# One block's adjacency by four indirect transfers of GpSimd, its features by four transfers addressed from registers

## The chip, the core and the metric

The kernel runs on one core of a Trainium2 chip. The core has five engines, each with an instruction queue of its own: TensorE (PE in the profile; the loads of its weights are listed as PEld), VectorE (DVE), ScalarE (ACT), GpSimd (POOL) and SyncE (SP), which here only issues transfers. Sixteen DMA engines move data between the chip's memory (HBM) and the core's on-chip memory (SBUF); TensorE writes to PSUM. The engines run independently and wait for each other and for transfers at semaphores. The metric is the device time of one execution in microseconds.

## The reference

One layer of a message-passing network over 128 graphs of 64 nodes with 128 features each. For each ordered pair of nodes (i, j) a three-layer MLP makes a message from the two nodes' features; messages are summed over j where the adjacency has an edge; a second MLP updates each node.

```python
def _mlp(x, w0, b0, g0, be0, w1, b1, g1, be1, w2, b2):
    h = jax.nn.relu(x @ w0 + b0)
    h = _layernorm(h, g0, be0)
    h = jax.nn.relu(h @ w1 + b1)
    h = _layernorm(h, g1, be1)
    return h @ w2 + b2
...
pair_feats = jnp.concatenate([f_i, f_j], axis=-1)          # (128, 64, 64, 256)
messages = _mlp(pair_feats, msg_w0, ..., msg_b2)
messages = messages * coupling_matrix[..., None]           # adj: (128, 64, 64), 0 or 1
agg = jnp.sum(messages, axis=2)
upd_in = jnp.concatenate([part_feats, agg], axis=-1)
updated = part_feats + _mlp(upd_in, upd_w0, ..., upd_b2)   # x: (128, 64, 128)
```

About an eighth of the adjacency's entries are edges, so a kernel may work on edges alone.

## The kernel before

**Tiling.** The kernel lists the edges of each graph in slots, 640 per graph (`CAP`), and works on edges alone. Two graphs make a pair (64 pairs, `NP`), four pairs a block (16 blocks, `NB`, `PB` = 4). A chunk is 512 edges; a pair has 2.5 chunks, a block ten, the whole run 160 (`NCHK`). If a graph has too many edges, a dense path behind a flag computes everything again; with these inputs it isn't taken.

**A block's way.** Its adjacency `an` (128 partitions: two graphs of 64 rows; by 4 pairs by 64 columns) is loaded in `load_adj`, its features `xn` (128 partitions by 4 pairs by 128) in `load_x`. From `an`, VectorE counts edges along each row (`rank`, tile `rk`), and GpSimd works out each edge's place (`place`, `place_out`, tile `posall`). From `xn`, TensorE makes transposes (`turn_x`, tile `xnT`) and then two products per node, split into a low and a high part (`rows`, tiles `abl` and `abh`). For each pair the two selection matrices that say which nodes an edge joins are made: `node_rows` casts one on GpSimd (tile `i`), `marks` and `compare` make the other on TensorE and VectorE (tile `j`). Four transfers of `stack`, two `s<-i` and two `s<-j` (one of each per graph of the pair), put them together in a tile `s` with 128 partitions. `gather` multiplies `abl` and `abh` by `s` (tile `hps`), chunk by chunk, which gives the first layer's output for 512 edges. The rest of the MLP, the sums over edges (tiles `oh` and `w`, `ys`) and the node update (`uo`) follow; the features `xn` are used once more in `residual`, which adds them to the output. GpSimd also makes a seed `u` for the second layer of some chunks, which VectorE adds in `y`.

**What sets the order.** Each step is put in a list by `at(n, tag, fn, ...)` at a time of 144 units per chunk plus a correction from the table `WHEN`, and the list is sorted and written out in that order. Each engine runs its own instructions in that order; so does SyncE with the transfers. `load_adj` of block b is at 19 chunks ahead of the block, `load_x` at 12 ahead, with corrections. Blocks 0 and 1 are loaded ahead of the list; `load_adj` and `load_x` handle blocks 2 to 15, 14 calls each. A steady block takes about 29.35 us. In the rows of the profile that carry a line number, L719 is the adjacency load, L724 the feature load, L898 `stack`, L1018 the transposing transfer of `node_marks`, L1162 the store of the output, L933 `gather`, L908 `marks`, L819 `turn_x`, and L1621 the load of the flag into a register on each engine at the end.

Of the kernel before, what the change touches and what calls it, by code (L numbers as in the profile page):

```python
# [12 lines left out]
I32 = mybir.dt.int32  # L13
# [362 lines left out]
def tile_gnn(  # L376
# [40 lines left out]
    nc = tc.nc  # L417
    B, N, C = x.shape
    P = 128
# [5 lines left out]
    NP = B // 2  # L425
# [5 lines left out]
    PB = 4  # L431
# [12 lines left out]
    xf = x.rearrange("b n c -> (b n) c")  # L444
    of = out.rearrange("b n c -> (b n) c")
    adjp = adj.rearrange("(p g) i j -> (g i) p j", g=2)

    const = ctx.enter_context(tc.tile_pool(name="const", bufs=1))
# [25 lines left out]
    def load_first(b, q0, q1):  # L474
# [55 lines left out]
    nc.gpsimd.iota(slot, pattern=[[2, CAP]], base=1, channel_multiplier=0,  # L530
                   allow_small_or_imprecise_dtypes=True)

    posall = const.tile([P, 2, PB, 2, N], F16, name="posall")
    nc.vector.memset(posall, 0.0)
    ones_row = const.tile([1, P], F32, name="ones_row")
# [134 lines left out]
    def edge_path(es):  # L670
# [45 lines left out]

        def load_adj(b):
            an = blkp.tile([P, PB, N], F32, name="an", bufs=3)
            nc.sync.dma_start(an, adjp[:, b * PB:(b + 1) * PB, :])  # L719
            blocks[b]["an"] = an  # L720

        def load_x(b):
            xn = blkp.tile([P, PB, C], F32, name="xn", bufs=5)
            nc.sync.dma_start(xn, xf[b * PB * P:(b + 1) * PB * P, :]  # L724
                              .rearrange("(q p) c -> p q c", p=P))
            blocks[b]["xn"] = xn

        def rank(b):
# [454 lines left out]
        for b in range(NB):  # L1183
            o = b * CPB
            if b > 1:
                at(max(o - 19, 0), "", load_adj, b)
                at(max(o - 12, 0), "", load_x, b)
            if b > 0:
                r = max(o - 12, 1)
                at(max(o - 14, 0), "", rank, b)  # L1190
                at(r, "", count, b)
                at(r + 1, "", count_out, b)
                at(r + 1, "", degrees, b)
                at(max(o - 9, r + 1), "", place, b)
                at(r + 2 if b == 1 else o - 7, "", place_out, b)
                at(max(o - 7, 13), "", odd_weights, b)
                at(o - 4, "", turn_x, b)
                at(o - 3, "", turn_x_out, b)
            for half, n in ((0, o - 3 if b else -1), (1, o + 2 if b else 3)):
                if n >= 0:  # L1200
                    if b < 2:
                        at(n, f".{half}", rows, b, half)
                    elif half == 0:
                        at(o - 2, "", rows_both, b)
                    r = o - 1 if b > 1 else n + 1
                    at(r, f".{half}", rows_hi, b, half)
                    at(r, f".{half}", rows_lo, b, half)
        for b in reversed(range(NB)):
# [11 lines left out]
            for u, n, t, m0_at, xo_at in units:  # L1220
                v = u.tag
# [35 lines left out]
        for p in range(NP):  # L1257
# [16 lines left out]
            q, h = divmod(p, 2)  # L1274
# [33 lines left out]
        for n in range(NCHK):  # L1308
# [5 lines left out]
            if n >= LEAD:  # L1314
                i = n - LEAD if n < QC else n
# [4 lines left out]
            if n >= 1:  # L1320
                i = n - 1 if n < QC else n + 1
# [337 lines left out]
```

## Time and profile before

| | |
|---|---|
| time, median of 2 runs | 501.37 us (501.12 to 501.61) |
| time of the profiled execution | 501.05 us |
| its span, first to last instruction | 499.3 us |
| mean granted TensorE clock | 0.997 of full speed |
| data moved by DMA | 63.55 MB, mean 127 GB/s |

The span is what all rows of the trace are counted in; the time of an execution has a little around it. In a row of the timeline the first number is the start in microseconds from the span's start, the second the length; then engine, line, operation, tiles as out<-in, shapes and count. A number in brackets is the engine's idle time before the row, with what ended it. SPq is SyncE's queue: the length of its rows is that of the issue, not of the transfer. In the views of one line or one tile three numbers with strokes are the shortest, median and longest instruction in nanoseconds. In the list of transfers the last number is the median time from issue to landing. A row of the waits names who waited and for whom, then the sum in microseconds, how often, and the longest.

### The profile page before, as it was taken

How to read it: one execution, taken by the hardware profiler on the slowest of the kernel's cores; microseconds unless marked ns; L12 is line 12 of the kernel's file. 1: busy time of each engine (PE TensorE's matmuls, PEld its weight loads, DVE VectorE, ACT ScalarE, POOL GpSimd, SP SyncE). 2: the span in 40 equal slices, each digit the busy share in tenths (PEclk: the TensorE clock that was granted, in tenths of full speed). 3: DMA queues.
4: the chain of work that ended last, by engine and by line, in shares of the span. 5: the costliest groups of instructions: out<-in, count | busy, mean ns of one | idle time of the engine just before them, and what ended most of it. 6: DMA issues, size and time to landing. Idle time of an engine off the chain costs nothing.

```text
span 499.3 us, 15949 instructions
## 1 busy us (share of the span) xinstructions
PE 486.1 (97%) x5947; PEld 460.6 (92%) x5947; DVE 468.0 (94%) x1225; ACT 397.1 (80%) x907; POOL 349.1 (70%) x563
## 2 busy tenths in 40 slices
PE   7999999999999999999999999999999999999996
PEld 4889999999999999989999998999989999999995
DVE  7999999999999999999999999999999998989985
ACT  6989978878787887868878786887868779867845
POOL 3275776967949776696877859776696859555771
PEclk9999999999999999999999999999999999999998
DMA  4766838376564756646486673666655458626231
GB/s 122 152 140 152 183 100 162 82 165 153 125 139 98 139 142 150 148 113 142 97 167 142 125 152 90 136 137 147 142 122 135 95 120 163 145 68 154 59 41 47
DMA packets 91474, 63.55 MB, mean 127 GB/s; under 512 B 57473, under 2 KB 75522, under 8 KB 91394
## 3 DMA queue, kind: packets, MB, share of 16 engines
q1 hardware_dynamic: 91106, 62.36, 57.7%
q8 instruction: 49, 0.80, 0.7%
q14 instruction: 31, 0.25, 0.2%
q10 hardware_dynamic: 288, 0.13, 0.1%
HBM read 7.15 MB, written 4.19 MB: 23 GB/s over the span
## 4 chain that ended last, share of the span: by engine, by line


## 5 line engine op out<-in xcount | busy, mean ns | idle before, releaser
L986 PE MATMUL z<-w1c,h 128*128 128x128 f32 x1280 | 190.1, 275 | 0.0
L986 PEld LDWEIGHTS z<-w1c,h 128*128 128x128 f32 x1280 | 172.4, 192 | 4.1 <-DVE uy_st L629 0.2
L938 ACT ACTIVATE h<-hps,b0c 128x512 f32<-128x512 f32 x160 | 108.9, 681 | 35.0 <-PE hps L933 34.5
L629 DVE BATCH_NORM_STATS2 st<-hT 128x6 f32<-128x256 f32 x320 | 122.4, 415 | 6.7 <-PE hT L943 5.1
L629 DVE BATCH_NORM_STATS2 st<-y 128x6 f32<-128x256 f32 x320 | 126.9, 418 | 1.6 <-ACT y L997 1.5
L980 ACT ACTIVATE z<-b1b,m_sd 128x128 f32<-128x128 f32 x320 | 117.3, 368 | 9.4 <-DVE y L613 3.7
L943 PE MATMUL hT<-ident,h 128*128 128x128 f32 x640 | 113.0, 276 | 1.9 <-DVE st L629 1.8
L933 PE MATMUL hps<-s,abl 128*128 128x512 f32 (+3 forms) x256 | 96.9, 381 | 2.6 <-ACT h L938 2.2
L933 PE MATMUL hps<-s,abh 128*128 128x512 f32 (+3 forms) x256 | 89.9, 358 | 0.0
L973 POOL TENSOR_TENSOR u<-b1b,m_sd 128x512 f32<-128x512 f32 x80 | 84.3, 1057 | 7.7 <-ACT m_sd L637 7.7
L943 PEld LDWEIGHTS hT<-ident,h 128*128 128x128 f32 x640 | 75.9, 141 | 6.3 <-issue 3.1
L1029 POOL TENSOR_TENSOR w<-oh,m_q 128x192 f32<-128x192 f16 x126 | 62.0, 513 | 8.8 <-DVE m_q L658 2.5
L916 DVE TENSOR_TENSOR j<-mk,cmpt 128x320 fp32r<-128x320 f32 x124 | 59.2, 477 | 6.3 <-PE mk L908 3.6
L891 POOL CAST i<-tp 128x640 fp32r<-128x640 f16 x58 | 41.7, 719 | 32.1 <-DMA s<-i 30.1
L997 ACT ACTIVATE y<-z 128x512 f32<-128x512 f32 x80 | 47.4, 595 | 17.7 <-PE z L986 17.3
L613 DVE CUSTOM_DVE_ANT_0 y<-z,u 128x512 f32<-128x512 f32 x80 | 54.0, 675 | 3.6 <-PE z L986 3.3
L933 PEld LDWEIGHTS hps<-s,abl 128*128 128x128 f32 x256 | 48.8, 191 | 7.7 <-ACT h L938 3.7
L876 ACT ACTIVATE d<-slot,mid 128x640 f16<-128x640 f16 x64 | 52.1, 818 | 1.7 <-POOL mid L765 1.0
L933 PEld LDWEIGHTS hps<-s,abh 128*128 128x128 f32 x256 | 49.1, 192 | 0.2
L647 POOL TENSOR_TENSOR m_v<-m_v,st 128x20 f32<-128x20 f32 x31 | 7.2, 232 | 58.5 <-DVE st L629 57.3
L1044 PE MATMUL ys<-y,w 128*32 128x128 f32 x1488 | 44.1, 274 | 0.0
L1044 PEld LDWEIGHTS ys<-y,w 128*32 128x32 f32 x1488 | 39.6, 110 | 2.5 <-issue 2.1
(193 smaller groups left out, 890.7 us busy)
## 6 DMA issues: line engine op xcount, KB each, us to landing
s<-i SPq DMA_DIRECT2D x124, 160.0 KB, 3.1
s<-j SPq DMA_DIRECT2D x124, 160.0 KB, 2.9
xn<-in_x_dram SPq DMA_DIRECT2D x15, 256.0 KB, 3.9
out_dram<-uo SPq DMA_DIRECT2D x15, 256.0 KB, 2.5
an<-in_adj_dram SPq DMA_DIRECT2D x16, 128.0 KB, 3.4
oh<-tp SPq DMA_TRANSPOSE x64, 3.2
xn<-in_x_dram SPq DMA_DIRECT2D x2, 128.0 KB, 3.0
out_dram<-uo SPq DMA_DIRECT2D x2, 128.0 KB, 2.0
```

Of the source, the lines that this page charges most:

```text
L613: nc.vector._custom_dve(TENSOR_ADD_SAT, out=o, in0=ps, in1=sb, s0=BIG, s1=0.0)
L629: nc.vector.bn_stats(st, src.rearrange("p t c -> p c t"))
L876: nc.scalar.activation(D[p], slot, AF.Abs, bias=blocks[b]["mid"][:, q:q + 1], scale=-1.0)
L916: nc.vector.tensor_tensor(JR[p][:, c], MK.pop((p, k))[:, 0:HC], cmpt[:, c], op=ALU.is_equal)
L933: nc.tensor.matmul(HP[n][:, c:c + w], lhsT=blocks[g // (2 * PB)]["ab", g // 4 % 2][k][:, g % 4, :], rhs=S[g // 2][:, g % 2, e:e + w], star ...
L938: nc.scalar.activation(H[n], HP.pop(n), AF.Relu, bias=b0c)
L943: nc.tensor.transpose(HT[n][:, t, :], H[n][:, t * P:(t + 1) * P], ident)
L973: nc.gpsimd.tensor_tensor(U[n], bc(W["b1b"], CH), SR[q][:, k:k + CH].unsqueeze(2).to_broadcast([P, CH, C]), op=ALU.mult)
L980: nc.scalar.activation(z_of(n)[:, t, :], W["b1b"], AF.Copy, scale=SR[q][:, k:k + 1])
L986: nc.tensor.matmul(ps[:, t, :], lhsT=H[n][:, t * P:(t + 1) * P], rhs=W["w1c"], start=by_vector(n) and t == 0, stop=True, skip_group_check= ...
L1029: (nc.vector if p == NP - 2 else nc.gpsimd).tensor_tensor(WT[p][:, g], oh, qs, op=ALU.mult)
L1044: nc.tensor.matmul(YS[b][g * N + m * HN:g * N + (m + 1) * HN, k, :], lhsT=w[:, g, m, u, :], rhs=y, start=(u == 0), stop=(u == TH - 1), til ...
```

## The change

Two tables of row numbers are made at the start by GpSimd: `row_at` holds, for partition p and pair r, the row 128 r + p of the adjacency seen as 8192 rows of 64; `at_row` holds the numbers 0 to 63 in one partition. `load_adj` then issues, instead of one load by SyncE, four indirect transfers by GpSimd, one per pair, each of which fetches 128 rows of 256 bytes by the indices in one column of `row_at`. `load_x` loads each of four numbers from `at_row` into a register of SyncE and issues four transfers of 64 KB, whose source address comes from the register. The data, the tiles and their places are the same. Blocks 0 and 1 are loaded as before.

```diff
@@ -530,6 +530,10 @@
     nc.gpsimd.iota(slot, pattern=[[2, CAP]], base=1, channel_multiplier=0,
                    allow_small_or_imprecise_dtypes=True)
 
+    row_at = const.tile([P, NP], I32, name="row_at")
+    nc.gpsimd.iota(row_at, pattern=[[P, NP]], base=0, channel_multiplier=1)
+    at_row = const.tile([1, NP], I32, name="at_row")
+    nc.gpsimd.iota(at_row, pattern=[[1, NP]], base=0, channel_multiplier=0)
     posall = const.tile([P, 2, PB, 2, N], F16, name="posall")
@@ -716,13 +720,20 @@
         def load_adj(b):
             an = blkp.tile([P, PB, N], F32, name="an", bufs=3)
-            nc.sync.dma_start(an, adjp[:, b * PB:(b + 1) * PB, :])
+            for q in range(PB):
+                nc.gpsimd.indirect_dma_start(
+                    out=an[:, q, :], out_offset=None, in_=adj.rearrange("b i j -> (b i) j"),
+                    in_offset=bass.IndirectOffsetOnAxis(
+                        ap=row_at[:, b * PB + q:b * PB + q + 1], axis=0))
             blocks[b]["an"] = an
 
         def load_x(b):
             xn = blkp.tile([P, PB, C], F32, name="xn", bufs=5)
-            nc.sync.dma_start(xn, xf[b * PB * P:(b + 1) * PB * P, :]
-                              .rearrange("(q p) c -> p q c", p=P))
+            for q in range(PB):
+                v = nc.sync.value_load(at_row[0:1, b * PB + q:b * PB + q + 1], min_val=0,
+                                       max_val=NP - 1)
+                nc.sync.dma_start(xn[:, q:q + 1, :],
+                                  xf.rearrange("(r p) c -> p r c", p=P)[:, bass.ds(v, 1), :])
             blocks[b]["xn"] = xn
```

SyncE's queue where block 7's features are loaded (160.37 us in the trace), before. The numbers behind `i` and `j` tell one pair's tiles from another's.

```order
L898 DMA s<-j_3034 64x640
L898 DMA s<-i_2902 64x640
L724 DMA xn<-in_x_dram 128x4x128
L898 DMA s<-j_3034 64x640
L719 DMA an<-in_adj_dram 128x4x64
L1018 DMA_TRANSPOSE oh<-tp 128x5x128
L898 DMA s<-i_3265 64x640 x2
```

And now, at the same place; the line numbers are 11 higher from `load_adj` on.

```order
L909 DMA s<-j_3251 64x640
L909 DMA s<-i_3119 64x640
L733 TENSOR_LOAD at_row
L733 ISA x2
L735 ISA
L735 DMA xn<-in_x_dram 128x128
...
L735 DMA xn<-in_x_dram 128x128
L909 DMA s<-j_3251 64x640
L1029 DMA_TRANSPOSE oh<-tp 128x5x128
L909 DMA s<-i_3524 64x640 x2
```

Between the two transfers `s<-j` of one pair stands now four times the group of a register load, two instructions on its value (a FUSED_REGOPS and a SEQ_ASSERT), one on the address and a DMA, and the load of `an` behind them is gone.

GpSimd's queue at the same place (161.10 us in the trace), before:

```order
L647 TENSOR_TENSOR um_v<-um_v,uy_st 128x4
L891 CAST i_3151<-tp 128x640
L1029 TENSOR_TENSOR w<-oh,m_q 128x192 x3
L891 CAST i_3265<-tp 128x640
L1029 TENSOR_TENSOR w<-oh,m_q 128x192
L863 CAST abh<-ab 128x512
```

And now:

```order
L651 TENSOR_TENSOR um_v<-um_v,uy_st 128x4
L902 CAST i_3368<-tp 128x640
L1040 TENSOR_TENSOR w<-oh,m_q 128x192
L724 DMA an<-in_adj_dram,row_at 128x64 x4
L1040 TENSOR_TENSOR w<-oh,m_q 128x192 x2
L902 CAST i_3524<-tp 128x640
L1040 TENSOR_TENSOR w<-oh,m_q 128x192
```

The four indirect transfers of block 8's adjacency stand behind the first of three products `w`.

GpSimd's queue at the start of the run, now. Before, `pos` and `posall` (the places of block 0's pairs 1 to 3) follow `slot` directly, and `cumall` follows them.

```order
L530 IOTA slot 128x640
L534 IOTA row_at 128x64
L536 IOTA at_row 1x64
L724 DMA an<-in_adj_dram,row_at 128x64 x4
L810 TENSOR_TENSOR pos<-rk,before 128x192
L815 TENSOR_TENSOR posall<-pos,an 64x3x64 x2
L724 DMA an<-in_adj_dram,row_at 128x64 x4
L760 TENSOR_SCALAR cumall<-raw 128x4
```

The transfers of block 2 stand ahead of block 0's places, those of block 3 behind them.

## The prediction

> **What bounds the kernel now.** I read the page's busy shares first, then the busy time by stretch, then who waited for whom on TensorE.
>
> ```profile
> span 499.3 us, 15949 instructions
> PE 486.1 (97%) x5947; PEld 460.6 (92%) x5947; DVE 468.0 (94%) x1225; ACT 397.1 (80%) x907; POOL 349.1 (70%) x563
> ...
> 158.00:187.35 29.35, 29.35 (x372) 28.39 (x370) 28.59 (x75) 23.92 (x55) 22.31 (x36) 1.00 0.62 136
> ...
> PE hps L933 <- ACT h L938: 2.2, 5, 0.7
> PE ma L819 <- DMA xn<-in_x_dram: 0.4, 1, 0.4
> ```
>
> The third line is one block in the steady part (columns: stretch, length, busy time and instruction count of PE, PEld, DVE, ACT and POOL, granted clock, DMA share and GB/s). TensorE is busy for 29.35 of 29.35 us at full clock. Over the whole run it idles 499.3 - 486.1 = 13.2 us, and its largest wait sums to 2.2 us. So TensorE sets the pace, it has no gaps in which to catch up, and whatever stops it for a microsecond lengthens the run by about a microsecond. Transfers cost nothing as long as they land before TensorE asks for them. The question is whether they still do.
>
> All transfers of the steady part leave from SyncE, in order. Its own waits and one block of its queue:
>
> ```profile
> SPq L898 <- DVE j L916: 95.3, 22, 8.1
> ...
> 158.84 0.46 SPq L898 DMA_DIRECT2D s<-j  x1
> 159.34 0.60 SPq L898 DMA_DIRECT2D s<-i  x1
> 160.37 0.38 SPq L724 DMA_DIRECT2D xn<-in_x_dram  x1
> 160.81 0.55 SPq L898 DMA_DIRECT2D s<-j  x1
> 161.43 0.57 SPq L719 DMA_DIRECT2D an<-in_adj_dram  x1
> 162.04 1.39 SPq L1018 DMA_TRANSPOSE oh<-tp  x1
> 163.55 1.78 SPq L898 DMA_DIRECT2D s<-i  x3
> 167.50 0.46 SPq L898 DMA_DIRECT2D s<-j  x1
> 173.85 0.39 SPq L1162 DMA_DIRECT2D out_dram<-uo  x1
> ```
>
> SyncE stands idle much of the time (95.3 us waiting for VectorE's `j` alone), but the feature load stands between the two halves of one pair's `s<-j`: the first at 158.84, the second at 160.81. The second half, the last rows of that pair's selection matrix, is what the next gather needs. How much time it has, for the first steady block, this one and the last: its issue, the load before it, and the first gather that reads it (by the number of matmul columns, graph 15, 47 and 103).
>
> ```profile
> 46.09 0.58 SPq L724 DMA_DIRECT2D xn<-in_x_dram  x1
> 46.72 0.59 SPq L898 DMA_DIRECT2D s<-j  x1
> 52.58 0.22 PE L933 MATMUL hps<-s,abl 128*128 128x128 f32 x1
> ...
> 167.35 0.22 PE L933 MATMUL hps<-s,abl 128*128 128x128 f32 x1
> ...
> 368.93 0.54 SPq L724 DMA_DIRECT2D xn<-in_x_dram  x1
> 369.52 0.57 SPq L898 DMA_DIRECT2D s<-j  x1
> 377.21 0.22 PE L933 MATMUL hps<-s,abl 128*128 128x128 f32 x1
> ...
> s<-j SPq DMA_DIRECT2D x124, 160.0 KB, 2.9
> ```
>
> From issue to gather: 5.86, 6.54 and 7.69 us, mean 6.7. A transfer lands 2.9 us after issue (last line, median). That leaves 6.7 - 2.9 = 3.8 us by which SyncE may be later before TensorE stands still.
>
> **The change part by part.** *The feature load, four times from a register.* Per quarter SyncE now runs a TENSOR_LOAD, two instructions of its value's bounds, one for the address, and a DMA. The kernel before has one such load, of the flag at its end:
>
> ```profile
> L1621 SPq TENSOR_LOAD <-flag x1: 738/738/738, 475.4 to 475.4; - x1
> L1621 SPq FUSED_REGOPS  x1: 183/183/183, 476.2 to 476.2; - x1
> L1621 SPq SEQ_ASSERT  x1: 37/37/37, 476.4 to 476.4; - x1
> L1621 POOLq TENSOR_LOAD <-flag x1: 490/490/490, 492.5 to 492.5; - x1
> ```
>
> One quarter: 0.74 + 0.18 + 0.04, the address as another FUSED_REGOPS 0.18, a DMA issue 0.50 (between 0.38 and 0.60 in the rows above), and five steps of 0.05 from one instruction to the next (160.37 + 0.38 to 160.81 is 0.06): 1.89 us, and 7.56 us for four. The one load took 46.72 - 46.09 = 0.63. So the second `s<-j` is issued 6.93 us later. Bounds of a quarter: 0.49 for the load (the POOL row), 0.10 for the address, 0.38 for the DMA and short steps, 1.39 us; above, a register load dearer again by the ratio of these rows, 0.74 x 0.74 / 0.49 = 1.11, and a DMA of 0.60, 2.36 us. I take 1.89, since the SP row is the same instruction on the same engine.
>
> [...]
>
> 6.93 against a cover of 3.8: TensorE stops for 3.1 us in each steady block. That is 12 blocks (features of blocks 3 to 14): 37.6 us. The stop can't be made up, since TensorE has no gaps. It doesn't grow either: SyncE is free again at about 171.3 instead of 165.3, the `s<-j` of 167.50 goes out 3.8 us late while TensorE runs 3.1 us late, and its gather, next fence, had 171.74 - 167.50 - 2.9 = 1.3 us in hand. By the `out` at 173.85, which waits for VectorE, SyncE has caught up. So it starts afresh in each block.
>
> Two loads lie elsewhere. Block 2's features are already waited for:
>
> ```profile
> 171.74 0.48 PE L933 MATMUL hps<-s,abl 128*128 128x512 f32 x1
> ...
> 32.54 0.58 SPq L724 DMA_DIRECT2D xn<-in_x_dram  x1
> ...
> 36.51 0.66 PE L819 MATMUL ma<-ident,xn 128*128 128x128 f32 x4 [0.44 <-DMA xn<-in_x_dram]
> ```
>
> The last quarter's DMA goes out at 32.54 + 3 x 1.89 + 1.39 = 39.6 and lands at about 42.5; its transposition, the fourth, began at about 36.8: 5.7 us, in which the late `s<-j` behind it is covered. Block 15's load stands apart, in the last stretch; I price it at nothing, and if that is wrong it costs no more than one of the twelve, 3 us.
>
> *The adjacency, four indirect transfers of GpSimd.* SyncE loses one issue of 0.6 us, after the late `s<-j`: no gain. When the adjacency lands doesn't matter: the load of 161.43 is first read by VectorE's scan at 182.37 (next fence), 21 us on, which covers any of the costs below, and the bytes are the same. What matters is that POOL runs the four inside its queue, after the first `w`. Their price is in no row. Below, 0.38 us each as SyncE's plain issue; above, 1.69 us, the longest POOL operation of the block (`xo`, last line below). I take 1.2, nearest to the dearest DMA issue: 4.8 us a block.
>
> ```profile
> 161.10 1.45 POOL L1029 TENSOR_TENSOR w<-oh,m_q 128x192 f32<-128x192 f16 x3
> 165.56 1.04 POOL L973 TENSOR_TENSOR u<-b1b,m_sd 128x512 f32<-128x512 f32 x1
> 170.11 0.23 POOL L647 TENSOR_TENSOR m_v<-m_v,st 128x20 f32<-128x20 f32 x1 [3.27 <-DVE st L629]
> ...
> 169.88 0.67 DVE L613 CUSTOM_DVE_ANT_0 y<-z,u 128x512 f32<-128x512 f32 x1
> 182.37 1.18 DVE L731 TENSOR_TENSOR_SCAN rk<-first,an 128x256 f16<-128x256 f32 x1
> ...
> 182.95 1.69 POOL L1087 TENSOR_TENSOR xo<-xn,cu2b 128x512 f32<-128x512 f32 x1
> ```
>
> The tightest user of what is queued behind them is VectorE's `y` at 169.88, whose `u` ends at 166.60: 3.3 us in hand, and 3.1 more since TensorE is late: 6.4. 4.8 fits, and the 3.27 us of POOL's idle time plus the same 3.1 take the rest. Without SyncE's stop 4.8 would cost 1.5 us a block.
>
> *At the start* the two new iotas and block 2's four transfers stand on POOL ahead of the places of block 0:
>
> ```profile
> 2.65 0.67 POOL L530 IOTA slot<- 128x640 f16 x1
> 5.66 0.51 POOL L799 TENSOR_TENSOR pos<-rk,before 128x192 f32<-128x192 f16 x1 [2.35 <-DVE before L784]
> 6.24 1.23 POOL L804 TENSOR_TENSOR posall<-pos,an 64x192 f16<-64x192 f32 x2
> 10.10 0.30 PE L908 MATMUL mk<-tp,posall 128*128 128x320 f16 x1
> ```
>
> POOL is free at 3.32; iotas of a tenth of the width 0.3, transfers 4.8, places 7.47 - 5.66 = 1.8: 10.2 against the marks of pair 1 at 10.10. With 0.1 us from one of the four transfers to the next, 0.5 us.
>
> The sum: 501.05 us for the profiled execution (span 499.3 and 1.75 around it; the median of the two runs shown, 501.37, is 0.3 above) + 37.6 + 5.7 + 0.5 = 545 us.
>
> **The rivals.** *Light registers.* The quarter costs its lower bound, 1.39: SyncE is 4.93 us late, TensorE stops 1.1 a block (13.6 in all), block 2 costs 3.7: 519 us. For it speaks that the load took 0.49 on other engines; against it, that SyncE's own took 0.74.
>
> *POOL becomes the bound.* The transfers hold POOL longer than the 6.4 us, from 1.6 us each on. At 2.2 (the 1.69 and one VectorE instruction of 0.5 waited out each time) `u` is 8.8 - 6.4 = 2.4 us late in 12 blocks, 29 us, and the start 4 us: 578 us. [...] Against it: POOL has 29.35 - 22.31 = 7.0 us idle in the block. [...]
>
> *Hidden after all (not slower).* SyncE's idle time takes the loads. It decides at 4 quarters = 3.8 + 0.63, 1.1 us a quarter, so only if the register load runs beside the DMAs around it. Then block 2's 2.6 us and the start remain: 504 us. Against it: the DMA needs the register's value, and the queue is in order behind the `j` wait. A gain isn't in reach: the DMA waits of TensorE that could go are 0.4 us.
>
> **How the numbers follow.** Forecast 0.70 (its own range, quarters of 1.6 to 2.3 us, the upper bound but for 0.06: 530 to 566), light registers 0.12, POOL 0.12, hidden 0.06. A measurement tells about 2%, 10 us, from no change, and three of the four cases lie beyond it: slower 0.93, same 0.06, faster 0.01. The range reaches from the light case, 519, to POOL's, 578; it leaves out the hidden case and about half of the tails beyond these two, some 0.15.
>
> **What would show it.** Right: SyncE's groups show 56 TENSOR_LOADs of about 0.74 us, the second `s<-j` of the pair issued about 7 us later than its first `s<-i`, and TensorE's waits show 12 stops of about 3 us on the DMA `s<-j`, with one of 5 to 6 us on `xn` near 37 us. POOL's transfers would show 1.2 us each and no wait of VectorE for `u`. Wrong: gathers that don't wait for `s<-j` (hidden); waits of VectorE's `y` for `u`, or POOL without idle time (POOL the bound); or SyncE's DMAs with a register far from 0.5 us each.

## The result and the profile after

The changed kernel takes 532.24 us (median of 2 runs, 531.73 to 532.75) against 501.37 before: the ratio is 1.0616, its 95% interval 1.0566 to 1.0665. It is slower by 30.9 us, less than the 43.6 us forecast. In the tables below, an execution that took over 1.5% longer than the fastest of its kernel counts in the median, but not in the ratio and its interval.

From the page of the changed kernel: span, busy shares, the granted clock in 40 slices, and the group of the indirect transfers.

```profile
span 530.8 us, 16371 instructions
PE 496.5 (94%) x5947; PEld 463.9 (87%) x5947; DVE 472.1 (89%) x1225; ACT 398.3 (75%) x907; POOL 406.0 (76%) x621
PEclk9899899999999999999999999999999999999999
L724 POOL DMA_INDIRECT an<-in_adj_dram,row_at x56 | 54.6, 974 | 15.1 <-issue 11.5
```

TensorE now idles 530.8 - 496.5 = 34.3 us instead of 13.2. Its busy time also grew, by 10.4 us: part of it is that the clock was halved in two stretches (0.50 from 12.82 to 16.24 us and from 60.60 to 64.02, the two 8s in PEclk), of which more below. What TensorE waits for:

```profile
PE hps L944 <- DMA s<-j: 9.1, 11, 2.0
PE mk L919 <- POOL posall L815: 2.4, 1, 2.4
```

The transfers `s<-j` are what it waits for most, as forecast; but the stops are 2 us at most, not 3. What the steps cost on SyncE, from the views of the two lines of the feature load:

```profile
L733 SPq TENSOR_LOAD <-at_row x56: 263/270/732, 34.8 to 448.6; - x56
...
L735 SPq FUSED_REGOPS  x56: 42/42/48, 35.8 to 449.1; - x56
...
L735 SPq DMA_DIRECT2D xn<-in_x_dram x56: 337/338/654, 36.0 to 449.3; - x56
```

One block of SyncE's queue, the one that the prediction shows for before (there at 158.84 to 173.85 us; here everything is 16.5 us later):

```profile
175.35 0.46 SPq L909 DMA_DIRECT2D s<-j  x1
175.87 0.59 SPq L909 DMA_DIRECT2D s<-i  x1
177.60 4.14 SPq L735 DMA_DIRECT2D xn<-in_x_dram  x4
181.78 0.62 SPq L909 DMA_DIRECT2D s<-j  x1
...
184.89 1.75 SPq L909 DMA_DIRECT2D s<-i  x3
186.73 0.54 SPq L909 DMA_DIRECT2D s<-j  x1
```

The same stretch on GpSimd, and the two gathers of TensorE that wait in it:

```profile
178.28 1.04 POOL L724 DMA_INDIRECT an<-in_adj_dram,row_at  x1 [0.15 <-issue]
...
182.12 0.94 POOL L724 DMA_INDIRECT an<-in_adj_dram,row_at  x1 [0.30 <-issue]
...
184.00 0.87 POOL L902 CAST i<-tp 128x640 fp32r<-128x640 f16 x1
...
184.49 0.33 PE L944 MATMUL hps<-s,abl 128*128 128x128 f32 x1 [0.44 <-DMA s<-j]
...
190.81 0.47 PE L944 MATMUL hps<-s,abl 128*128 128x512 f32 x1 [1.55 <-POOL cumall L760]
```

The first gather, behind the feature load, waits 0.44 us: SyncE was held, the second `s<-j` went out at 181.78. The other, the first gather of the next block, waits 1.55 us, and this stop isn't in the prediction. (Its row names `cumall`, which is no operand of it; the profile names the latest event on GpSimd's semaphore. The operand `s` comes from the `s<-j` of 186.73, issued 4.08 us earlier. At 11 other stops the row names `s<-j`.) Go back along it: that `s<-j` stands behind three `s<-i`, which left at 184.89, the moment the cast `i` of 184.00 + 0.87 = 184.87 was done. That cast stands on GpSimd behind the four indirect transfers. Before, the same cast was done at 163.21, and the `s<-i` left at 163.55, right behind the transposition ahead of them:

```profile
162.49 0.72 POOL L891 CAST i<-tp 128x640 fp32r<-128x640 f16 x1
```

So one chain leads from GpSimd's queue over SyncE's queue to TensorE. By the start of each graph's first gather, after less before, the stop behind the feature load grew by 5.5 us in the eleven blocks 2 to 12 (0.5 a block), and the stop at the next block's first gather by 16.6 us (1.5 a block). Block 1, in which block 3's features are loaded, lost more at these two places, 2.2 and 1.6 us. The start gave 2.8 us, block 2's features 1.65. Together that is 30.3 of the 30.8 us by which the last graph's first gather came later.

### The profile page after: what moved, and what is told of

It is laid out like the page before. It is cut to its first block, busy times and chain, and to the rows that moved or that the text cites. A ratio compares the mean times of both kernels' runs of the same rounds, so it can differ in the third digit from the quotient of the medians.

```text
span 530.8 us, 16371 instructions
## 1 busy us (share of the span) xinstructions
PE 496.5 (94%) x5947; PEld 463.9 (87%) x5947; DVE 472.1 (89%) x1225; ACT 398.3 (75%) x907; POOL 406.0 (76%) x621
## 4 chain that ended last, share of the span: by engine, by line
## 5 line engine op out<-in xcount | busy, mean ns | idle before, releaser
L944 PE MATMUL hps<-s,abl 128*128 128x512 f32 (+3 forms) x256 | 98.4, 387 | 20.1 <-DMA s<-j 9.1
L724 POOL DMA_INDIRECT an<-in_adj_dram,row_at x56 | 54.6, 974 | 15.1 <-issue 11.5
L893 DVE TENSOR_SCALAR tp<-d,deg 128x640 f16<-128x640 f16 x64 | 42.6, 665 | 1.3 <-ACT d L887 1.1
```

Source lines behind the costliest of these rows:

```text
L724: nc.gpsimd.indirect_dma_start(out=an[:, q, :], out_offset=None, in_=adj.rearrange("b i j -> (b i) j"), in_offset=bass.IndirectOffsetOnAxi ...
L944: nc.tensor.matmul(HP[n][:, c:c + w], lhsT=blocks[g // (2 * PB)]["ab", g // 4 % 2][k][:, g % 4, :], rhs=S[g // 2][:, g % 2, e:e + w], star ...
```

## The experiments

**First, the parts one at a time.** Features alone:

```diff
         def load_adj(b):
-            for q in range(PB):
-                nc.gpsimd.indirect_dma_start(
...
+            nc.sync.dma_start(an, adjp[:, b * PB:(b + 1) * PB, :])
```

> Features by four register-addressed transfers of SyncE, adjacency by SyncE's one load as before. Three theories. T1, SyncE alone: both stops of a block (about 0.6 us at the second s<-j behind the feature load, about 1.5 us at the next block's first gather) come from SyncE being held by the register groups, and GpSimd's transfers cost only the 2.8 us at the start. T1: 532.2 - 2.8 = about 529 us. T2, a chain over two queues: the first stop is SyncE's hold, the second is GpSimd's cast i standing behind the indirect transfers, so that SyncE's s<-i and the s<-j behind it go out late. T2: 501.4 + 1.7 (block 2) + 8 (first stops) + at most 6 left of the second stops = 511 to 517 us, and the first gather of a block waits less than 0.5 us more than before. T3, contention: the s<-j lands later because the four indirect transfers move beside it, whatever the times of issue: about 512 us too, so this run tells T1 from T2 and T3 only.

Adjacency alone:

```diff
         def load_x(b):
-            for q in range(PB):
-                v = nc.sync.value_load(at_row[0:1, b * PB + q:b * PB + q + 1], min_val=0,
-                                       max_val=NP - 1)
...
+            nc.sync.dma_start(xn, xf[b * PB * P:(b + 1) * PB * P, :]
+                              .rearrange("(q p) c -> p q c", p=P))
```

> Adjacency by four indirect transfers of GpSimd, features by SyncE's one load as before. T1 (SyncE alone): 501.4 + 2.8 at the start = about 504 us. T2 (cast i behind the transfers, then SyncE's s<-i and s<-j): SyncE's s<-i goes out after the late cast, about 3 us later than before, of which the s<-j behind it has 2 us of pause to take up; stop of about 1 us per block, 504 + 12 = 512 to 520 us, with SyncE waiting for the cast i ahead of s<-i in each block. T3 (contention): stop of the same size with the s<-j issued when it was before, landing 1 us later or more: 512 to 520 us.

Four transfers without registers, with the adjacency as in the first edit:

```diff
         def load_x(b):
             for q in range(PB):
-                v = nc.sync.value_load(...)
                 nc.sync.dma_start(xn[:, q:q + 1, :],
-                                  xf.rearrange("(r p) c -> p r c", p=P)[:, bass.ds(v, 1), :])
+                                  xf.rearrange("(r p) c -> p r c", p=P)[:, b * PB + q:b * PB + q + 1, :])
```

> Features by four plain transfers of SyncE at fixed addresses, no registers; adjacency by SyncE's one load as before; no tables of row numbers. Tells the registers from the splitting into four. All three theories: SyncE is held 4 x 0.6 us in place of one issue of 0.6, 1.9 us more, which is under the 3.8 us of cover: 501 to 503 us, no stop of TensorE beyond those of before. If splitting the load is the cost, not the register work: 509 to 517, as feat_only.

The indirect transfers at another place in GpSimd's queue:

```diff
-    "load_adj": {1: -693, 102: -349, 103: -1531},
+    "load_adj": {1: -570, 102: -349, 103: -1531},
```

> The changed kernel with one number of the order's table moved, so that the four indirect transfers stand on GpSimd behind the second cast i, the products w, abh, abl and u, instead of ahead of them; all else as in the changed kernel. T1 (SyncE alone): 532 us, no change. T2 (cast i late): the second stops shrink from 18 us in sum to at most 6, so 518 to 522 us, and SyncE's s<-i at the block's end goes out right behind the register groups without a wait for GpSimd. T3 (contention of transfers): the transfers move by about 4 us and run beside the s<-j of the next pair still more: 532 or above.

Measured, with the ratio to before of each group of runs and its 95% interval. The steady part is measured by ten blocks, from the first gather of graph 24 (block 3) to that of graph 104 (block 13); before, they take 298.03 us.

| kernel | us | ratio (interval) | ten blocks, us | more per block, us |
|---|---|---|---|---|
| the change | 532.24 | 1.0616 (1.0566 to 1.0665) | 316.75 | 1.87 |
| features alone | 521.98 | 1.0407 (1.0373 to 1.0440) | 312.06 | 1.40 |
| adjacency alone | 534.55 | 1.0655 (1.0611 to 1.0698) | 320.21 | 2.22 |
| four transfers, no registers | 501.86 | 1.0008 (0.9989 to 1.0028) | 298.44 | 0.04 |
| adjacency behind `u` | 524.81 | 1.0422 (1.0343 to 1.0501) | | |

The ten blocks are read from two rows of TensorE's timeline each: of before,

```profile
83.58 0.51 PE L933 MATMUL hps<-s,abl 128*128 128x512 f32 x1
381.61 0.48 PE L933 MATMUL hps<-s,abl 128*128 128x512 f32 x1
```

of the changed kernel,

```profile
95.21 0.47 PE L944 MATMUL hps<-s,abl 128*128 128x512 f32 x1 [1.74 <-DMA s<-j]
411.96 0.47 PE L944 MATMUL hps<-s,abl 128*128 128x512 f32 x1 [0.35 <-ACT uhT L1110]
```

of the features alone,

```profile
91.50 0.47 PE L938 MATMUL hps<-s,abl 128*128 128x512 f32 x1 [1.55 <-DMA s<-j]
403.56 0.47 PE L938 MATMUL hps<-s,abl 128*128 128x512 f32 x1 [0.41 <-ACT uhT L1104]
```

and of the adjacency alone.

```profile
94.00 0.47 PE L939 MATMUL hps<-s,abl 128*128 128x512 f32 x1 [1.42 <-ACT y L1003]
414.21 0.47 PE L939 MATMUL hps<-s,abl 128*128 128x512 f32 x1 [0.65 <-ACT uhT L1105]
```

Two surprises. The parts alone cost 20.7 and 33.3 us (less before's 501.28 in those runs), together 54, while the whole change costs 31. And the adjacency alone, which every theory put at 520 or below, costs about as much as both. T1 falls: SyncE isn't alone in it. T2 has the right chain, but it puts both parts alone too low (511 to 517 and 512 to 520), and it wrongly adds the two holds, that is, the times for which the new work keeps SyncE's and GpSimd's queues. With the adjacency behind `u` the interval, 518.5 to 526.4 us, reaches into T2's 518 to 522 and shuts out the 532 of T1 and T3. Splitting the feature load into four isn't the cost; the register groups are.

In the features alone SyncE holds itself up: the `s<-i` leave behind its own queue (here 12.4 us later than before up to this block), and the next pair's `s<-j` behind them.

```profile
177.10 0.50 SPq L903 DMA_DIRECT2D s<-j  x1
...
179.67 1.79 SPq L903 DMA_DIRECT2D s<-i  x3
181.55 0.54 SPq L903 DMA_DIRECT2D s<-j  x1
```

Before, that `s<-j` left at 167.50 + 12.4 = 179.9 on this scale: 1.65 us are lost, though SyncE had a pause there before (165.3 to 167.50). By itself that would fit: 171.74 - 167.50 - 2.5 = 1.7 us were in hand with the landing time that this one transfer had before. But it also landed later after its issue. It now follows three transfers of its size without a pause, which is the likely reason; no run tested that by itself. From the view of the line, this one transfer before, and then in the features alone:

```profile
DMA to landing us min/median/max: 2.5/2.5/2.5
```

```profile
DMA to landing us min/median/max: 4.3/4.3/4.3
```

1.65 later and 1.8 slower, less 1.7, make about 1.7 us; the first gather of the block (graph 48) moved by 1.8 against the one ahead of it. So the later landing has a share in the size of the stop. If it is crowding, as T3 has it, the transfers that crowd are the `s<-i`, not GpSimd's: this kernel has none of those.

In the adjacency alone SyncE is ready early and stands waiting for the cast:

```profile
178.69 1.30 SPq L1024 DMA_TRANSPOSE oh<-tp  x1
185.81 2.01 SPq L904 DMA_DIRECT2D s<-i  x3
187.93 0.53 SPq L904 DMA_DIRECT2D s<-j  x1
```

Its waits put numbers on it. Each row is named for `w`, the product behind the cast that releases it. First the adjacency alone, then the changed kernel, then before:

```profile
SPq L904 <- POOL w L1035: 76.2, 14, 6.6
```

```profile
SPq L909 <- POOL w L1040: 27.5, 14, 3.0
```

```profile
SPq L898 <- POOL w L1029: 7.3, 10, 3.0
```

In the changed kernel SyncE waits less for the same cast, since it spends that time on its register groups. This gave theory T4: the two holds run at the same time, the later one decides, and the indirect transfers matter only as time in GpSimd's queue.

**Second, T4 against its rivals.** GpSimd held by other work, with no indirect transfer and no register; the eight additions are extra work whose result nobody uses, and both loads are SyncE's as before:

```diff
         def load_adj(b):
-            for q in range(PB):
-                nc.gpsimd.indirect_dma_start(
...
+            nc.sync.dma_start(an, adjp[:, b * PB:(b + 1) * PB, :])
+            for q in range(2 * PB):
+                nc.gpsimd.tensor_tensor(busy, busy, busy, ALU.add)
```

> No indirect transfers and no registers: adjacency and features by SyncE's single loads as before; where the changed kernel issues a block's four indirect transfers, GpSimd does eight additions of a 128x288 tile to itself that nobody uses (extra work, about 8 x 0.65 = 5.2 us a block beside the 4 x 1.25 = 5.0 us of the transfers). Theory T4, formed after the first four runs: GpSimd's queue is held, its cast i behind the held place is late, SyncE's three s<-i wait for it, and the next pair's s<-j goes out behind them; nothing of it is special to transfers. T4: 525 to 536 us, as with the indirect transfers alone (534.6). Theory T3, it is the transfers (their movement, or the making of their descriptors): 502 to 506 us.

The register groups moved into SyncE's idle time:

```diff
-    "load_x": {8: -290, 102: 631, 115: 184},
+    "load_x": {8: -350, 102: 631, 115: 184},
```

> The changed kernel with one number of the order's table moved, so that the feature load's register groups stand ahead of the s<-j for which SyncE waits some 7 us in each block, in SyncE's idle time; the indirect transfers stay where the change put them. T4 adds that the two holds run at the same time (SyncE's groups about 5 us, GpSimd's transfers about 5 us, both between the same two casts), so that the stop is as long as the later of the two and not their sum: with SyncE's hold gone, GpSimd's remains, 528 to 535 us, near the indirect transfers alone (534.6), SyncE waiting for the cast i ahead of the three s<-i. T2 (the two in series, each adding its own): the first stops and SyncE's part of the second go, 532.2 - 8 - 6 = about 518 to 524 us.

Both tables' numbers moved (-570 and -350):

> The changed kernel with both numbers moved: the register groups in SyncE's idle time, the four indirect transfers behind the second cast i, the products w, abh, abl and u of GpSimd. T4 and T2 alike: neither hold is in the way of an s<-i or s<-j, so what is left is the start (2.8 us), block 2's features (1.7 us) and small remainders: 504 to 509 us. If the transfers themselves or the registers cost time wherever they stand (T3): 515 or above.

The same, and the start as before:

```diff
+            if b < 4:
+                nc.sync.dma_start(an, adjp[:, b * PB:(b + 1) * PB, :])
-            for q in range(PB):
+            for q in range(PB if b >= 4 else 0):
```

> As the run with both numbers moved, and the adjacency of blocks 2 and 3 (eight of the 56 indirect transfers, which stand among block 0's places on GpSimd) is loaded by SyncE as before. If the 2.4 us that TensorE waits for posall near 10 us come from these transfers: 2 to 3 us less than with both numbers moved, 501 to 506 us, and no half-clock window near 13 us. If they come from the two tables of row numbers (the iotas): within 1 us of it.

The ten blocks are read from the same two gathers in each trace.

| kernel | us | ratio (interval) | ten blocks, us | more per block, us |
|---|---|---|---|---|
| GpSimd held by additions | 545.37 | 1.0893 (1.0843 to 1.0943) | 327.54 | 2.95 |
| register groups moved | 534.41 | 1.0640 (1.0610 to 1.0670) | 317.65 | 1.96 |
| both moved | 522.85 | 1.0431 (1.0397 to 1.0466) | 304.77 | 0.67 |
| both moved, start as before | 519.42 | 1.0377 (1.0335 to 1.0420) | 303.29 | 0.53 |

The additions do what the transfers do, and more: 545.37 lies above even T4's 525 to 536. GpSimd and SyncE's wait there:

```profile
179.90 5.89 POOL L723 TENSOR_TENSOR busy<-busy 128x288 f32<-128x288 f32 x8
...
186.75 0.71 POOL L895 CAST i<-tp 128x640 fp32r<-128x640 f16 x1
...
SPq L902 <- POOL w L1033: 77.8, 14, 6.5
```

They hold GpSimd for 5.89 us, the transfers for 182.12 + 0.94 - 178.28 = 4.78, and TensorE's clock was halved more often (six times in the ten blocks against none in the changed kernel, last section). Nothing of an indirect transfer is needed for a loss of this size; the theory that it is the transfers (T3) falls. With the register groups out of the way the loss per block stays (1.96 against 1.87), and SyncE waits for the cast again as long as with the adjacency alone:

```profile
SPq L909 <- POOL w L1040: 75.5, 14, 6.8
```

That is what T4 said, and the series theory T2 (518 to 524) did not. The run with both moved was a miss for both: 522.85 in place of 504 to 509. Its stops at `s<-j` are gone, but the transfers, now ahead of GpSimd's `m_v`, make that late. The group on GpSimd, and who waits, in this kernel:

```profile
176.05 1.03 POOL L724 DMA_INDIRECT an<-in_adj_dram,row_at  x1 [0.15 <-issue]
...
180.85 0.31 POOL L650 TENSOR_SCALAR m_v<-st 128x20 f32<-128x20 f32 x1
...
ACT m_sq L657 <- POOL m_v L651: 30.2, 25, 2.7
```

Before, that wait of ScalarE was

```profile
ACT m_sq L653 <- POOL m_v L647: 11.6, 12, 1.7
```

and GpSimd idled 3.27 us between the two `m_v` and 2.58 us ahead of another cast:

```profile
178.91 0.72 POOL L891 CAST i<-tp 128x640 fp32r<-128x640 f16 x1 [2.58 <-DMA s<-i]
```

The late `m_v` is a likely part of the 0.67 us a block that are left; its share wasn't measured apart. No idle time of GpSimd in the block holds all four transfers, but each of these two holds two. With the start as before the time came to 519.42 instead of 522.85, not to the 501 to 506 that was expected; the two intervals overlap, so the times don't tell the two kernels apart. The traces do: the first gather of graph 2 stands 1.24 us later than in the kernel before with both moved, and in its old place with the start as before, so that the tables of row numbers cost nothing and the eight transfers do.

**Third, each hold in idle time.** Features alone with the groups moved (adjacency as before, -350):

> Register-addressed features alone (adjacency by SyncE's one load as before), with the register groups ahead of the s<-j for which SyncE waits some 7 us in a block. If SyncE's hold ahead of s<-j and s<-i is the whole cost of the registers in the steady part: the 20.7 us of the features alone shrink to the place of block 2's features (stops near 38 and 53 us, 3.4 + 1.8 + 1.0) and the waiting for GpSimd's xo ahead of the feature load: 503 to 509 us. If the registers or the 64-KB transfers cost time wherever they stand: 515 to 522 us.

Adjacency alone, two transfers ahead of `m_v` and two ahead of that cast; blocks 2 and 3 by SyncE:

```diff
+        def load_adj2(b):
+            if b >= 4:
+                fetch(b, 2)
+        def fetch(b, q0):
+            an = blocks[b]["an"]
+            for q in (q0, q0 + 1):
+                nc.gpsimd.indirect_dma_start(
...
-    "load_adj": {1: -693, 102: -349, 103: -1531},
+    "load_adj": {1: -570, 102: -349, 103: -1531},
+    "load_adj2": {1: 90, 102: -349, 103: -1531},
...
                 at(max(o - 19, 0), "", load_adj, b)
+                at(max(o - 19, 0), "", load_adj2, b)
```

> Indirect transfers alone (features by SyncE's one load as before), in two lots of two: two behind u, ahead of the m_v for whose statistics GpSimd idles 3.3 us in a block before the change, two ahead of the cast i for which it idles 2.6 us. Blocks 2 and 3 are loaded by SyncE as before, so 48 of the 56 transfers are left. T4 (GpSimd's queue is held, and each hold costs only what sticks out of GpSimd's own idle time): each lot takes 2.5 us, under the idle time in both places, so 501 to 505 us. If transfers of GpSimd cost time wherever they stand, as the run with both moved (522.9) could be read: 512 or above.

Both, with block 2's features by a plain load:

> Both parts at their new places: the register groups in SyncE's idle time, the indirect transfers in two lots in GpSimd's two idle times; block 2 and 3's adjacency and block 2's features by SyncE's plain loads as before (48 of 56 indirect transfers and 13 of 14 register-addressed feature loads are left). T4: 502 to 507 us, within 1% of before, with no half-clock window before the end. If the remainder of the run with both moved came from the registers: near 512 and above.

And block 3's features too:

> As the run with both parts spread (513.4), and block 3's features too are loaded by SyncE's one plain load (12 of 14 register-addressed feature loads and 48 of 56 indirect transfers are left). If the two stops near 50 and 58 us of that run (4.0 + 1.65 us) come from block 3's register groups, which stand there ahead of three s<-i with no idle time of SyncE: 506 to 509 us. If they come from the adjacency's transfers of block 4 at the same time: 512 to 514 us.

| kernel | us | ratio (interval) | ten blocks, us | more per block, us |
|---|---|---|---|---|
| features alone, moved | 509.02 | 1.0158 (1.0125 to 1.0191) | 298.94 | 0.09 |
| adjacency alone, spread | 506.52 | 1.0088 (1.0056 to 1.0120) | 298.79 | 0.08 |
| both, spread | 513.37 | 1.0222 (1.0176 to 1.0267) | 302.09 | 0.41 |
| both, spread, block 3 plain | 509.22 | 1.0166 (1.0145 to 1.0187) | 301.27 | 0.32 |

The same instructions of the steady part, moved, cost 0.09 instead of 1.40 us a block on SyncE and 0.08 instead of 2.22 on GpSimd. The times came out at the end of the expected range (features, 503 to 509) and above it (adjacency, 501 to 505), but well below the 515 and 512 of the rivals. Both together still cost 0.41 and 0.32, more than the sum of the two; why wasn't settled. The register groups where they now stand, in the features alone, and two of the transfers ahead of `m_v`, in the adjacency alone, spread:

```profile
156.63 1.19 SPq L903 DMA_DIRECT2D s<-j  x2
161.10 4.42 SPq L729 DMA_DIRECT2D xn<-in_x_dram  x4
165.63 0.50 SPq L903 DMA_DIRECT2D s<-j  x1
```

```profile
169.23 0.95 POOL L735 DMA_INDIRECT an<-in_adj_dram,row_at  x1 [0.30 <-issue]
170.21 0.30 POOL L649 TENSOR_SCALAR m_v<-st 128x20 f32<-128x20 f32 x1
171.34 0.23 POOL L650 TENSOR_TENSOR m_v<-m_v,st 128x20 f32<-128x20 f32 x1 [0.83 <-DVE st L632]
```

After the transfers GpSimd still waits 0.83 us for VectorE. Of the 7.3 us that the moved features still cost, 5.4 arise at block 2, whose load stands where SyncE has no idle time. With both parts spread the time, 513.37, missed T4's 502 to 507 and came to its rival's 512 or above, by which the register groups make the rest. One stop of 4.0 us and one of 1.65 us were left, at 53 and 58 us; with block 3's features loaded plainly they are gone, and the loss, each against before in its own runs, falls from 11.6 to 8.5 us. So they came from the register groups, not from block 4's adjacency, though the time ended a little above the expected 506 to 509. The last kernel keeps 48 of 56 indirect transfers and 12 of 14 register-addressed loads and is 8.5 us slower than before. Its remainder is spread over waits of about 1 us and less, most in the second half of the run; what makes it up wasn't settled. No kernel tried beats the one before.

## Why the prediction was right, and where not

- *TensorE is the bound, each stop lengthens the run, and transfers made late on SyncE make the stops:* right. The time lies in the range (519 to 578) and in the forecast's own range (530 to 566), but the terms behind it were partly wrong and made up for each other, so that its closeness is in part luck.
- *A quarter of the feature load costs 1.89 us, 7.56 for four:* too dear. The register load was priced by the single one of the flag, 0.74; the median here is 0.27, below every price that the prediction had for it, the longest 0.73. The DMA took 0.34, the address 0.04. The second `s<-j` left 181.78 - 175.87 = 5.91 us after the `s<-i`, before 1.47: 4.4 us later and not 6.93. Less the cover of 3.8 that is 0.6, and 0.5 a block was measured. The reckoning with the cover held; the price of a step didn't. It lies even below the rival of light registers (4.93 late, 1.1 a block).
- *"It doesn't grow either", since the next `s<-j` had 1.3 us in hand:* this is the step that failed. It looked at SyncE's delay alone and left out that the three `s<-i` ahead of it wait for GpSimd's cast. That stop is the larger one, 1.5 us a block.
- *The four transfers cost 1.2 us each and 4.8 a block:* right, 4.78 (0.94 and 0.30 between two). *They fit, since the tightest user queued behind them is VectorE's `y`, with 6.4 us:* wrong. The tightest user was the cast `i`, whose result SyncE's queue waits for. GpSimd's queue as shown ahead of the prediction had it: the transfers stand between two casts. For the adjacency alone the prediction named 1.5 us a block over `u`; 2.2 came, over the cast.
- *POOL becomes the bound (from 1.6 us a transfer, 578):* half right. GpSimd's hold did decide the larger stop, at 1.25 us a transfer, and by another user than the rival named. No run shows the 0.5 us of a VectorE instruction in its 2.2 us a transfer: the 56 took 0.94 us in the median and 1.51 at most.
- *The start, 0.5 us:* 2.8. TensorE waited 2.4 us for `posall` behind the transfers, and the clock was halved after it (0.50 from 12.82 to 16.24 us). *Block 2's features, 5.7 us:* 1.65 in the changed kernel, on top of the late start; 5.4 in all with the features alone, moved.
- *Sum:* 37.6 for the steady stops was forecast as one stop of 3.1 in each of 12 blocks; there are two, of 0.5 and 1.5 in blocks 2 to 12 and more in block 1. Over the twelve blocks the stop that was forecast came to 7.6 us, and the one that was put at nothing to 18.2, some 26 us in all.

## What to carry to other kernels

An engine's idle share, or even its idle time in the very block, doesn't pay for an instruction added ahead of something that another queue waits for (GpSimd idled 7.0 of 29.35 us in the block, and the adjacency alone cost 2.22): list what stands behind the new work on its engine, and for each of its results the whole queue that stops for it (here a cast, three transfers, and the fourth behind them). The holds on the two queues that meet at one consumer here didn't add: the later decided, so that taking SyncE's alone away won nothing (534.41 us with the register groups moved, 532.24 with both holds), and the parts measured alone sum to more than the whole (54 us against 31). Either part's instructions, put into idle stretches as long as themselves, if need be in two lots, cost almost nothing in the steady part (0.09 and 0.08 us a block); both parts together still cost 0.3 to 0.4 us a block.

## What the runs showed of the hardware that was not expected

A stop of TensorE cost more than its length where the granted clock went to 0.50 after it. Two stops, the first in the adjacency alone, the second with the register groups moved (stretch, length, busy time of PE, PEld, DVE, ACT and POOL, granted clock, DMA share, GB/s):

```profile
190.22:193.63 3.41, 1.42 (x10) 1.34 (x11) 2.37 (x8) 1.13 (x3) 3.16 (x8) 1.00 1.16 145
193.63:197.04 3.41, 3.41 (x18) 3.27 (x17) 3.01 (x9) 2.60 (x9) 2.20 (x4) 0.50 0.51 138
```

```profile
189.53:192.94 3.41, 1.64 (x14) 1.45 (x13) 1.99 (x5) 1.97 (x4) 2.18 (x5) 1.00 1.11 181
192.94:196.36 3.42, 2.90 (x24) 2.79 (x24) 2.99 (x10) 1.67 (x5) 3.17 (x8) 1.00 0.55 106
```

The first stop, of 2.22 us, ended at 192.21. At 193.63 the clock went to half, for 3.41 us, which loses up to 1.7 us more. The second, of 2.29 us, ended at 193.46, and the clock stayed full. The shorter stop of 1.55 us in the changed kernel (190.81) wasn't followed by a halved stretch either.

The traces show what tells these stops apart. The starts of the halved stretches in one trace lie whole multiples of 3.413 us apart: with the adjacency alone at 63.92, 125.36, 159.50 and 193.63, which is 18, 10 and 10 of them; in the changed kernel at 12.82 and 60.60, 14 of them. Cut the ten blocks of each trace into pieces of that length, counted from these starts. In the ten of these pieces that stand right ahead of a halved stretch TensorE idled for 1.96 to 2.68 us, in all others for 1.88 at most. So in the steady part it was not the length of a stop that decided, but how much idle time fell into one piece: 2.0 of the 2.22 us did, while the stop of 2.29 us was cut in two, 1.77 and 0.5. Outside the ten blocks, in the kernel before, a piece with 1.82 us of idle time (492.98 to 496.40) was followed by a halved stretch too, so idle time alone doesn't give the whole rule.

Within the ten blocks the trace has three such stretches for the adjacency alone, one with the register groups moved, six with the additions, none in the changed kernel. At 1.7 us each, the most that one can lose, the loss per block without them is 2.22 - 0.51 = 1.7, 1.96 - 0.17 = 1.8, 2.95 - 1.02 = 1.9, and 1.9. So at this price the three halved stretches account for the adjacency alone being no cheaper, per block, than both parts together.

A register load from SBUF on SyncE took 0.27 us in the median of 56 and 0.73 at most, so the one such load in a trace, 0.74, is a poor price for many.
